# Turning keys on VectorE and through DRAM instead of on TensorE, in a four-block transformer kernel

## The chip, the cores and the metric

One core of a Trainium2 chip runs the whole program. The core has five engines with instruction streams of their own: TensorE (PE, matmuls; its weight loads are shown as PEld), VectorE (DVE), ScalarE (ACT), GpSimd (POOL) and SyncE (SP). SP computes nothing; it issues most of the DMAs, in order. TensorE reads SBUF and writes PSUM (8 banks of 128 partitions x 512 floats); the other engines bring results out of PSUM.

The metric is device time in microseconds (us). The kernel before takes 925.78 us (median of three runs, 925.47 to 926.54).

## The reference

The input x is 2 batches of 1024 tokens with 512 features, in float32. Four blocks follow each other, each applied to the layer-normed running sum and added to it:

1. attention a: 4 heads of 128, in chunks of 128 tokens (the stage that the change touches most);
2. a gated feed-forward net (called f in the kernel), 512 to 1408 to 512, whose weights are integer codes;
3. attention b: full softmax attention over 1024 tokens;
4. the same feed-forward net once more (called g).

Attention a, cut to what matters, for each batch, chunk and head:

```
q, k, v = x@Wq + bq, x@Wk + bk, x@Wv + bv
k = k / max(|k|, 1e-12)
attn  = (q k^T) * beta^T * decay        # decay is causal, from cumulative log gates
y     = attn v  +  (q state^T) * chunk_decay
state = state * total_decay + v^T (k * beta * decay_to_end)
```

The product q k^T contracts over the 128 features of a head. TensorE contracts over partitions, so the keys, which come out of their projection with tokens on partitions, are needed a second time with features on partitions: kT, a 128x128 transpose for each head.

## The kernel before, in words

**Tiling.** The 2048 tokens are 16 tiles (t = 0 to 15) of 128 tokens, and 4 groups (st = 0 to 3) of 4 tiles. Matmul inputs that need float32 accuracy are cut into a high and a low part, hi by a ScalarE cast and lo by a VectorE subtraction (`split`, L73), and multiplied in three matmuls (`mm3`, L88).

**Attention a** is the loop over t from L749. One turn does, in the order of the code: one head of the queries of a later group (`q_head`, L500, four turns ahead, so turns 0 to 11 have one and 12 to 15 have none); the keys and values of tile t+1 (`kv_tile`, L577, which calls `kv_part` for Wk and for Wv); and `scores(t)` (L617). `scores` turns the keys of tile t with four TensorE transposes into one PSUM bank (pkT, L622), copies them to SBUF with ScalarE (kT, L624), squares the keys of t+1 for their norm (`k_norm`), does the state's products (pd, L635), finishes tile t-1 (`chunk_out`: pl, L668, and pg, L673), and multiplies kT by the queries (pS, L650). Every fourth turn has the gates' projection as well (`gate_proj`, pc). The tiles kT and the keys (sWk) have two buffers each.

**Layer norms.** Groups 0 and 1 of attention a are turned by TensorE (`layernorm_T`). All later norms (groups a2, a3, f0 to f3, b0 to b3 and g0 to g3, 14 groups in all) go another way: `ln_norm` (L188) normalises a tile and turns its 32x32 blocks with VectorE (L198) into the tile y, which has one buffer; `ln_move` (L201) then puts the blocks on their partitions with 16 DMAs for each group, from SBUF to SBUF, each of 32 partitions x 16 x 32 floats (L209). The groups a, f, b0, b1, half of b2 and g3 are issued by SP, the others by POOL. `ln_split` (group a) and `combine` (the others) then read the turned group and make the matmul inputs, in slots of a pool of 12 (`slot`, L50). In `ln_split` the low part is written over the turned group.

The same kind of move through DRAM already stands in attention b: the probabilities are turned in 32x32 blocks by VectorE (L1100), written to DRAM by one DMA (L1104) and read back by four DMAs that put the blocks in place (L1116).

**What sets the order.** The code's order gives priorities. A planner with its own model of times then orders each engine's instructions and SP's DMAs ahead of the run, and puts in the waits; on the chip every engine and every DMA queue runs its list strictly in that order. `behind(...)` and `tc.issue_after(...)` add orders by hand: what is in their block comes after a given instruction of the same engine. `key_copy` holds such an instruction, the ScalarE copy of kT: the decay of tile t+1 (`decay`, ScalarE and POOL), the casts of groups a2 and a3 (`a_split`, at t = 3 and 7) and the squares of `k_norm` stand behind it.

**The end of attention a.** From t = 12 the loop also prepares the next block: `combine("f", 0)` in `moving` (subtractions L257, splits L76), the weight product V (its operands are loaded at L82 and split; pV), and the first feed-forward weights. The feed-forward net's products are pX, pY, pZ and pV with the suffix f or g.

Of the kernel before, what the change touches and what calls it, by code (L numbers as in the profile page):

```python
# [16 lines left out]
P = 128  # L17
D = 512
KD = D // P
# [15 lines left out]
def hybrid_block_kernel(ctx: ExitStack, tc: tile.TileContext, a, out):  # L35
# [14 lines left out]
    def slot(name, dt=F32R):  # L50

        return wp.tile([P, 2048], dt, tag="slot", name=name)
# [20 lines left out]
    def split(hi, lo, src, eng=None):  # L73

        c = nc.scalar.copy(hi, src)  # L75
        return c.ins, (eng or nc.vector).tensor_tensor(lo, src, hi.bitcast(F32), ALU.subtract).ins  # L76
# [61 lines left out]
    x_in = a["x"]  # L138
    x1 = [dp.tile([P, D], F32, tag=f"x1_{t}", name=f"x1_{t}") for t in range(NT)]
    x2 = [dp.tile([P, D], F32, tag=f"x2_{t}", name=f"x2_{t}") for t in range(NT)]  # L140
    x3 = [dp.tile([P, D], F32, tag=f"x3_{t}", name=f"x3_{t}") for t in range(NT)]
    cl_d = [dp.tile([16, P], F32, tag=f"cl_{g}", name=f"cl_{g}") for g in range(NST)]
    p_d = [dp.tile([T // P, P, P], F32, tag=f"p_{i}", name=f"p_{i}") for i in range(NC)]
# [39 lines left out]
            low.dma_start(out=dst[m][:, 512:1024], in_=lo.bitcast(F32))  # L183
        return done

    lnT, lnY, lnX, laid = {}, {}, {}, []

    def ln_norm(src, nm, st, i):  # L188

# [10 lines left out]

    def ln_move(nm, st, b):  # L201

        if b == 0:
            lnT[nm, st] = slot(f"xT_{nm}{st}").rearrange("p (k c) -> p k c", k=KD)
        y = lnY[nm, st]
        xf = lnT[nm, st].bitcast(F32).rearrange("p k (i b q) -> p (k i) b q", i=ST, b=4)
        for c in range(4):
            sync = nm in "af" or (nm, st) in (("b", 0), ("b", 1), ("g", 3)) or ((nm, st) == ("b", 2) and c % 2)
            (nc.sync if sync else nc.gpsimd).dma_start(  # L209
                out=xf[32 * b : 32 * (b + 1), :, c, :],  # L210
                in_=y[32 * c : 32 * (c + 1), b].rearrange("p k i q -> p (k i) q"),
            )

    def ln_split(nm, st):

        def part(k):
            if k == 0:
                xl = lnT[nm, st]
                lnT[nm, st] = slot(f"xh_{nm}{st}").rearrange("p (k c) -> p k c", k=KD), xl
            xh, xl = lnT[nm, st]  # L220
            split(xh[:, k, :], xl[:, k, :], xl[:, k, :].bitcast(F32))

        return [lambda k=k: part(k) for k in range(KD)]

# [17 lines left out]
    def combine(nm, pr):  # L242


        B = {}

        def begin():
            ra, rb = (lnT[nm, 2 * pr + n].bitcast(F32) for n in range(2))
            B.update(B11=ra[:, 0:2], B12=rb[:, 0:2], B21=ra[:, 2:4], B22=rb[:, 2:4])

        def part(n, src):
            o = slot(f"{n}_{nm}{pr}").rearrange("p (s k c) -> p s k c", s=2, k=2)
            XT[nm, pr, n] = o
            split(o[:, 0], o[:, 1], B[src])

        def less(dst, x, y):
            nc.vector.tensor_tensor(B[dst], B[x], B[y], ALU.subtract)  # L257

        if nm == "b":

            return [
                lambda: (begin(), part("B11", "B11")),
                lambda: part("B21", "B21"),
                lambda: part("B12", "B12"),
                lambda: part("B22", "B22"),
                lambda: less("B11", "B12", "B11"),
                lambda: part("T1", "B11"),
                lambda: less("B12", "B22", "B12"),
                lambda: part("T3", "B12"),
                lambda: less("B22", "B22", "B11"),  # L270
                lambda: part("T2", "B22"),
                lambda: less("B21", "B21", "B22"),
                lambda: part("T4", "B21"),
            ]
# [73 lines left out]
    with ExitStack() as actx:  # L348
# [16 lines left out]

        wc = a1.tile([P, KD, 2, 384], F32R, name="wc")
        normed, key_copy, late_norm = {}, [], []
        xTa, za, gta, sca, qTa, kva, ata, deca, sta, rowa, facta = ({} for _ in range(11))
        wqkv = {}
        rows = a1.tile([P, 2 * D + 96], F32, name="rows")  # L370
        bk_b, bv_b, bab_b = rows[:, 0:D], rows[:, D : 2 * D], rows[:, 2 * D : 2 * D + 2 * H]
# [186 lines left out]
        def kv_part(t, nm):  # L558
            st, i = divmod(t, ST)
            xh, xl = xTa[st]  # L560
            cs = bass.ts(i, P)
            ps = psum(f"p{nm}{t}")
            n = 256 if nm == "Wv" else 512
            for k in range(KD):
                w = wqkv[nm][k]
                mm3(ps[:, 0:n], xh[:, k, cs], xl[:, k, cs], w[:, 0:n], w[:, n : 2 * n], k == 0, k == KD - 1)
            if nm == "Wv":
                o, b = av.tile([P, 2, P], F32, tag="sWv", name=f"sWv{t}"), bv_b[:, 0:256]
            else:
                o, b = tl("sWk", t), bk_b  # L570
            nc.vector.tensor_tensor(o.rearrange("p h d -> p (h d)"), ps[:, 0:n], b, ALU.add)
            kva[t] = (*kva.get(t, ()), o)
# [1 line left out]
        def value(t, h):  # L574
            return kva[t][-1][:, h, :] if h < 2 else vbs[0][:, t % 8, h - 2, :]

        def kv_tile(t):  # L577
            kv_part(t, "Wk")
            kv_part(t, "Wv")

        def k_norm(t, after=None):

            kf, v = kva[t]
            sq = tl("sq", t)
            ss = mp.tile([P, H], F32, tag="ss", name=f"ss{t}")
            with tc.issue_after(after) if after is not None else nullcontext():
                for h in range(H):
                    squared = nc.scalar.activation(
                        sq[:, h, :], kf[:, h, :], AF.Square, accum_out=ss[:, h : h + 1]
                    ).ins  # L590
            normed[t] = (squared,)
            if t == NT - 1:
                late_norm.append(lambda: k_factor(t, ss))
            else:
                k_factor(t, ss)
# [21 lines left out]
        def scores(t):  # L617
            st, i = divmod(t, ST)
            kf, kw, v = kva[t]
            pkT = psum(f"pkT{t}").rearrange("p (h c) -> p h c", h=H)  # L620
            for h in range(H):
                nc.tensor.transpose(pkT[:, h, :], kf[:, h, :], ident)  # L622
            kT = tl("kT", t)
            copied = nc.scalar.copy(kT, pkT).ins  # L624
            key_copy[:] = [copied]
            if t == 0:
                with behind((copied,)):
                    decay(0)
            if t + 1 < NT:
                k_norm(t + 1, copied)  # L630
            if kw is not None:
                ec = sca[st][1]
                pd = psum(f"pd{t}").rearrange("p (h c) -> p h c", h=H)
                for h in range(H):
                    nc.tensor.matmul(pd[:, h, :], kw[:, h, :], value(t, h), start=True, stop=True)  # L635
                new = tl("state", t, pool=av)
                if t % NC == 0:
                    nc.vector.tensor_copy(new, pd)
                else:
                    old = tl("sdec", t)  # L640
                    nc.gpsimd.tensor_tensor(
                        old, sta[t], ec[:, 2, i, :].unsqueeze(2).to_broadcast([P, H, P]), ALU.mult
                    )
                    nc.vector.tensor_tensor(new, pd, old, ALU.add)
                sta[t + 1] = new
            if t > 0:
                chunk_out(t - 1)
            pS = psum(f"pS{t}").rearrange("p (h c) -> p h c", h=H)
            for h in range(H):
                nc.tensor.matmul(pS[:, h, :], kT[:, h, :], qTa[st][:, h, bass.ts(i, P)], start=True, stop=True)  # L650
            at = tl("at", t)
            s1 = facta.pop(t)
            for h in range(H):
                weighed = nc.vector.scalar_tensor_tensor(
                    at[:, h, :], pS[:, h, :], s1[:, h : h + 1], deca[t][:, h, :], ALU.mult, ALU.mult
                ).ins
            ata[t] = at
            return weighed
# [66 lines left out]
                with behind((*normed_x, *copied)):  # L725
                    spill(ap, ("kT", "kw", "sdec", "at"), pm, m_d, "M")
        load_wv()
        kv_tile(0)
        decays(0)
        k_norm(0)  # L730

# [15 lines left out]
        moving = combine("f", 0)  # L747
        wcs, loads = [], []
        for t in range(NT):  # L749
            if t + 4 < NT:  # L750
                q_head(*divmod(t + 4, ST))
            if t == 0:
# [2 lines left out]
                load_row(1)  # L755
            load_row(t + 1)
            if t + 1 < NT:
                kv_tile(t + 1)
            weighed = scores(t)
            if t % ST == 0 and t + ST < NT:  # L760
                gate_proj(t // ST + 1)
# [40 lines left out]
                next(prep)  # L802
        next(prep)
        chunk_out(NT - 1)
        spilled = spill(ap, ("sq", "kT", "kw", "sdec"), next(prep)[0], vo_d, "V")


    def ffn(src, dst, nm, wcs, moving, ended, after):
# [532 lines left out]
```

## Time and profile before

| what | value |
|---|---|
| median of three runs | 925.78 us (925.47 to 926.54) |
| profiled execution, its own time | 925.62 us |
| its span, first to last instruction | 923.9 us |
| granted TensorE clock | 1.000 |
| PE busy | 918.3 us (99%), 4546 matmuls |
| DVE busy | 692.0 us (75%) |
| ACT busy | 434.1 us (47%) |
| POOL busy | 260.2 us (28%) |
| DMA packets | 216182, of them 151024 under 512 bytes |

The page of a profile gives the busy time of each engine, the span in 40 slices, the DMA queues, the chain of work that ended last, and the costliest groups of instructions. A group is a source line, an engine and an operation with its tiles; a mean is the time of one instruction from its start to its end. Matmuls overlap their neighbours, so what one costs in a row of them is the distance between starts and not its own duration. Further answers of the trace are used below: who waited for whom, one tile's instructions, the chain in order of time, and stretches of the timeline of one engine or queue. SPq is the queue of DMAs that SP issues. The time of a DMA has two parts: how long SP is taken up by issuing it, and how long after that the data have landed.

### The profile page before, as it was taken

To read this page: it belongs to the slowest core of one execution; us is meant where nothing else is said; L and a number is where in the kernel's file an instruction comes from. 1 tells how busy PE (TensorE), PEld (TensorE's weight loads), DVE (VectorE), ACT (ScalarE), POOL (GpSimd) and SP (SyncE) were. 2 spreads that over 40 slices of the span, in tenths; PEclk is the share of its full clock that TensorE was granted. 3 is DMA by queue.
4 is the path that set the end of the run, shared out by engine and by line. 5 is a ranking of instruction groups with operands and counts; after the bars stand their busy time and mean duration, and the time that the engine had idled before them with its cause. 6 is when DMAs were issued, how large, how long until landed. Compare 5 with 4: busy or idle time off the path is not lost.

```text
span 923.9 us, 13662 instructions
## 1 busy us (share of the span) xinstructions
PE 918.3 (99%) x4546; PEld 778.6 (84%) x4546; DVE 692.0 (75%) x1335; ACT 434.1 (47%) x928; POOL 260.2 (28%) x458
## 2 busy tenths in 40 slices
PE   9999999999999999999999999999999999999998
PEld 8899999998888888888888888888888888888887
DVE  7755657579998798788948878569978876977654
ACT  5645455556776434444234444145444444444431
POOL 4345334556563002212130401140501531001100
PEclk9999999999999999999999999999999999999999
DMA  9535655477979754724743779225969745454012
GB/s 324 190 104 123 208 160 152 145 209 272 370 223 329 214 177 156 212 49 139 278 99 77 171 175 260 71 43 130 247 144 366 241 146 137 165 206 140 20 69 80
DMA packets 216182, 162.20 MB, mean 176 GB/s; under 512 B 151024, under 2 KB 167728, under 8 KB 216112
## 3 DMA queue, kind: packets, MB, share of 16 engines
q1 hardware_dynamic: 212624, 150.05, 53.6%
q0 software_dynamic: 3488, 11.28, 4.6%
q8 instruction: 36, 0.59, 0.3%
q14 instruction: 34, 0.28, 0.1%
HBM read 104.76 MB, written 41.84 MB: 159 GB/s over the span
## 4 chain that ended last, share of the span: by engine, by line
PE 93%; DVE 2%; SPq 2%; DMA 2%; issue 1%; ACT 0%; POOL 0%; DVEq 0%; ACTq 0%
PE pog L925 4%; PE pog L924 4%; PE pXf L338 4%; PE pVg L338 4%; PE pXg L338 4%; PE pof L924 4%; PE pVf L338 4%; PE pZf L338 4%; PE pZg L338 4%; PE pof L925 4%; PE pob L90 3%; PE pob L89 3%; PE pob L91 3%; PE psZ L1023 2%; PE psV L1023 2%; PE psX L1023 2%
## 5 line engine op out<-in xcount | busy, mean ns | idle before, releaser
L924 PE MATMUL pog<-wdg,hsg 128*128 128x512 f32 (+1 forms) x165 | 60.1, 375 | 0.0
L925 PE MATMUL pog<-wdg,hsg 128*128 128x512 f32 (+1 forms) x165 | 60.0, 375 | 0.0
L925 PE MATMUL pof<-wdf,hsf 128*128 128x512 f32 x154 | 59.1, 389 | 0.0
L924 PE MATMUL pof<-wdf,hsf 128*128 128x512 f32 x154 | 58.9, 389 | 0.0
L76 POOL TENSOR_TENSOR hsg<-sgg,hsg 128x128 fp32r<-128x128 f32 x40 | 18.6, 486 | 112.7 <-ACT hsg L75 68.8
L89 PE MATMUL pob<-vh,pth 128*128 128x512 f32 x128 | 49.9, 390 | 0.0
L91 PE MATMUL pob<-vh,ptl 128*128 128x512 f32 x128 | 49.8, 389 | 0.0
L90 PE MATMUL pob<-vl,pth 128*128 128x512 f32 x128 | 49.8, 389 | 0.0
L338 PE MATMUL pVg<-T_g,wcg 128*128 128x512 f32 x176 | 46.4, 389 | 0.0
L338 PE MATMUL pVf<-T_f,wcf 128*128 128x512 f32 x176 | 46.2, 389 | 0.0
L338 PE MATMUL pXg<-B_g,wcg 128*128 128x512 f32 x176 | 46.2, 389 | 0.0
L338 PE MATMUL pXf<-B_f,wcf 128*128 128x512 f32 x176 | 45.7, 390 | 0.0
L113 POOL TENSOR_SCALAR ve_g<-mv_g 128x1 f32<-128x1 f32 x16 | 8.0, 508 | 128.5 <-DVE mv_g L111 128.4
L209 POOL DMA_DIRECT2D xT_g<-y_g x48 | 31.1, 657 | 36.1 <-DVE T_b L76 29.4
L338 PEld LDWEIGHTS pVf<-T_f,wcf 128*128 128x128 f32 x176 | 33.0, 188 | 6.9
L338 PEld LDWEIGHTS pXg<-B_g,wcg 128*128 128x128 f32 x176 | 33.0, 188 | 6.8
L338 PEld LDWEIGHTS pVg<-T_g,wcg 128*128 128x128 f32 x176 | 33.0, 188 | 6.9
L338 PEld LDWEIGHTS pXf<-B_f,wcf 128*128 128x128 f32 x176 | 33.0, 188 | 6.8
L545 ACT ACTIVATE row<-row,ncl 128x128 f32<-128x128 f32 x64 | 20.5, 391 | 34.2 <-POOL row L534 34.1
L113 POOL TENSOR_SCALAR ve_b<-mv_b 128x1 f32<-128x1 f32 x16 | 5.6, 352 | 109.7 <-DVE mv_b L111 109.6
L924 PEld LDWEIGHTS pog<-wdg,hsg 128*128 128x128 f32 x165 | 31.1, 188 | 5.6
L925 PEld LDWEIGHTS pog<-wdg,hsg 128*128 128x128 f32 x165 | 31.0, 188 | 5.6
(344 smaller groups left out, 2844.2 us busy)
## 6 DMA issues: line engine op xcount, KB each, us to landing
wcg<-wc SPq DMA_DIRECT2D x19, 896.0 KB, 5.1
wc<-wcf SPq DMA_DIRECT2D x11, 896.0 KB, 5.1
p<-py SPq DMA_DIRECT2D x15, 512.0 KB, 3.6
wcf<-wc SPq DMA_DIRECT2D x8, 896.0 KB, 6.2
ptl<-p SPq DMA_DIRECT2D x56, 128.0 KB, 3.0
xin_a<-in_x SPq DMA_DIRECT2D x16, 256.0 KB, 4.9
xra<-in_x SPq DMA_DIRECT2D x16, 256.0 KB, 3.3
row<-cl SPq DMA_DIRECT2D x16, 256.0 KB, 4.1
```

The lines of the kernel that those rows point to most:

```text
L76: return c.ins, (eng or nc.vector).tensor_tensor(lo, src, hi.bitcast(F32), ALU.subtract).ins
L89: nc.tensor.matmul(ps, lhs_hi, rhs_hi, start=first, stop=False)
L90: nc.tensor.matmul(ps, lhs_hi, rhs_lo, start=False, stop=False)
L91: end = nc.tensor.matmul(ps, lhs_lo, rhs_hi, start=False, stop=last).ins
L113: nc.gpsimd.tensor_scalar(ve, mv[:, 1:2], EPS, None, ALU.add)
L209: (nc.sync if sync else nc.gpsimd).dma_start(out=xf[32 * b : 32 * (b + 1), :, c, :], in_=y[32 * c : 32 * (c + 1), b].rearrange("p k i q -> ...
L338: nc.tensor.matmul(ps, w[:, m, k * P : (k + 1) * P], o[:, s, k, :], start=first and k == 0 and s == 0, stop=k == 1 and s == 1, skip_group_ ...
L545: nc.scalar.activation(row[:, h, :], row[:, h, :], AF.Exp, bias=ncl[:, n : n + 1], scale=-1.0)
L924: nc.tensor.matmul(ps, hs[i][0][:, j], wd[j][:, ds], start=j == 0, stop=False)
L925: nc.tensor.matmul(ps, hs[i][1][:, j], wd[j][:, ds], start=False, stop=j == KH - 1)
L1023: ends[nm] = nc.tensor.matmul(ps, o[:, i, k], w[:, j, k], start=first and k == 0 and i + j == 0, stop=k == 1 and i == 1, skip_group_check= ...
```

## The change: what it does

1. Keys of tiles 1 to 11 (`TURNED`): the four TensorE transposes and the ScalarE copy are replaced by `turn_key`: one VectorE transpose of 32x32 blocks into a tile ky, one DMA to DRAM (k_d) and four DMAs back into kT, all five issued by SP. Tiles 0 and 12 to 15 stay as they were.
2. `kv_tile` is taken apart. The keys of t+1 (`k_tile`, with `turn_key`) now stand at the start of turn t, ahead of the later group's `q_head`; the values stand where they stood.
3. `key_copy` holds the VectorE transpose for the turned tiles, and `k_norm` of t+1 is no longer ordered behind the ScalarE copy.
4. All 14 norm groups: `ln_move` writes a group to DRAM with four DMAs (SP) and reads it back with one (SP for a and f, POOL for b and g). The slot for the group is taken only at the read. The group lies in another order in its slot, so `ln_split` and `combine` read it in runs of 32 floats; `ln_split` writes into two new slots.
5. The tiles sq (squares, two buffers before) and ky have one buffer each, and the V spill uses the buffers of `at` in place of those of sq.

```diff
+    k_d = [dp.tile([H, P, P], F32, tag=f"k_{t}", name=f"k_{t}") for t in range(NT)]
...
     def ln_move(nm, st, b):
         if b == 0:
-            lnT[nm, st] = slot(f"xT_{nm}{st}").rearrange("p (k c) -> p k c", k=KD)
-        y = lnY[nm, st]
-        xf = lnT[nm, st].bitcast(F32).rearrange("p k (i b q) -> p (k i) b q", i=ST, b=4)
-        for c in range(4):
-            sync = nm in "af" or (nm, st) in (("b", 0), ("b", 1), ("g", 3)) or ((nm, st) == ("b", 2) and c % 2)
-            (nc.sync if sync else nc.gpsimd).dma_start(
-                out=xf[32 * b : 32 * (b + 1), :, c, :],
-                in_=y[32 * c : 32 * (c + 1), b].rearrange("p k i q -> p (k i) q"),
+            lnD[nm, st] = dp.tile([P, 4, 512], F32, tag=f"ln_{nm}{st}", name=f"ln_{nm}{st}")
+        d = lnD[nm, st]
+        nc.sync.dma_start(
+            out=d.rearrange("(b q) c f -> c q b f", b=4)[b],
+            in_=lnY[nm, st][32 * b : 32 * (b + 1)].rearrange("p b k i q -> p b (k i q)"),
+        )
+        if b == 3:
+            lnT[nm, st] = slot(f"xT_{nm}{st}")
+            (nc.sync if nm in "af" else nc.gpsimd).dma_start(
+                out=lnT[nm, st].bitcast(F32), in_=d.rearrange("p c f -> p (c f)")
             )
 
     def ln_split(nm, st):
         def part(k):
             if k == 0:
-                xl = lnT[nm, st]
-                lnT[nm, st] = slot(f"xh_{nm}{st}").rearrange("p (k c) -> p k c", k=KD), xl
-            xh, xl = lnT[nm, st]
-            split(xh[:, k, :], xl[:, k, :], xl[:, k, :].bitcast(F32))
+                lnD[nm, st] = lnT[nm, st].bitcast(F32).rearrange("p (c k i q) -> p k i c q", c=4, k=KD, i=ST)
+                lnT[nm, st] = new_xT(f"{nm}{st}")
+            hi, lo = (x[:, k].rearrange("p (i c q) -> p i c q", i=ST, c=4) for x in lnT[nm, st])
+            split(hi, lo, lnD[nm, st][:, k])
...
     def combine(nm, pr):
         def begin():
-            ra, rb = (lnT[nm, 2 * pr + n].bitcast(F32) for n in range(2))
-            B.update(B11=ra[:, 0:2], B12=rb[:, 0:2], B21=ra[:, 2:4], B22=rb[:, 2:4])
+            ra, rb = (
+                lnT[nm, 2 * pr + n].bitcast(F32).rearrange("p (c n q) -> p n c q", c=4, q=32) for n in range(2)
+            )
+            B.update(B11=ra[:, 0:8], B12=rb[:, 0:8], B21=ra[:, 8:16], B22=rb[:, 8:16])
         def part(n, src):
...
-            split(o[:, 0], o[:, 1], B[src])
+            split(*(o[:, s].rearrange("p k (i c q) -> p (k i) c q", i=ST, c=4) for s in range(2)), B[src])
...
-        def kv_tile(t):
+        def turn_key(t):
+            y = tl("ky", t, pool=a1)
+            turned = nc.vector.transpose(
+                y.rearrange("p h c -> p (h c)"), kva[t][0].rearrange("p h c -> p (h c)")
+            ).ins
+            key_copy[:] = [turned]
+            nc.sync.dma_start(out=k_d[t].rearrange("h p f -> p h f"), in_=y)
+            kTa[t] = kT = tl("kT", t)
+            placed = k_d[t].rearrange("h (c j) (r q) -> r j (h c) q", c=4, r=4)
+            for n in range(4):
+                nc.sync.dma_start(
+                    out=kT[32 * n : 32 * (n + 1)].rearrange("p h (c q) -> p (h c) q", c=4), in_=placed[n]
+                )
+
+        TURNED = range(1, NT - 4)
+
+        def k_tile(t):
             kv_part(t, "Wk")
-            kv_part(t, "Wv")
+            if t in TURNED:
+                turn_key(t)
 
         def k_norm(t, after=None):
             kf, v = kva[t]
-            sq = tl("sq", t)
+            sq = tl("sq", t, pool=a1)
...
         def scores(t):
             kf, kw, v = kva[t]
-            pkT = psum(f"pkT{t}").rearrange("p (h c) -> p h c", h=H)
-            for h in range(H):
-                nc.tensor.transpose(pkT[:, h, :], kf[:, h, :], ident)
-            kT = tl("kT", t)
-            copied = nc.scalar.copy(kT, pkT).ins
-            key_copy[:] = [copied]
+            if t not in TURNED:
+                pkT = psum(f"pkT{t}").rearrange("p (h c) -> p h c", h=H)
+                for h in range(H):
+                    nc.tensor.transpose(pkT[:, h, :], kf[:, h, :], ident)
+                kTa[t] = tl("kT", t)
+                key_copy[:] = [nc.scalar.copy(kTa[t], pkT).ins]
+            kT = kTa.pop(t)
             if t == 0:
-                with behind((copied,)):
+                with behind(key_copy):
                     decay(0)
             if t + 1 < NT:
-                k_norm(t + 1, copied)
+                k_norm(t + 1)
...
-        kv_tile(0)
+        k_tile(0)
+        kv_part(0, "Wv")
...
         for t in range(NT):
+            if t + 1 < NT:
+                k_tile(t + 1)
             if t + 4 < NT:
                 q_head(*divmod(t + 4, ST))
...
             if t + 1 < NT:
-                kv_tile(t + 1)
+                kv_part(t + 1, "Wv")
             weighed = scores(t)
...
-        spilled = spill(ap, ("sq", "kT", "kw", "sdec"), next(prep)[0], vo_d, "V")
+        spilled = spill(ap, ("at", "kT", "kw", "sdec"), next(prep)[0], vo_d, "V")
```

More of the change, by code (lines that the diff above doesn't have):

```diff
@@ L184, in spill @@
         return done
-    lnT, lnY, lnX, laid = {}, {}, {}, []
+    lnT, lnY, lnX, lnD, laid = {}, {}, {}, {}, []
     def ln_norm(src, nm, st, i):
@@ L367, in hybrid_block_kernel @@
         normed, key_copy, late_norm = {}, [], []
-        xTa, za, gta, sca, qTa, kva, ata, deca, sta, rowa, facta = ({} for _ in range(11))
+        xTa, za, gta, sca, qTa, kva, ata, deca, sta, rowa, facta, kTa = ({} for _ in range(12))
         wqkv = {}
```

## The prediction

> **What bounds the kernel now.** I read the page first: busy times, then the chain that ended last.
>
> ```profile
> PE 918.3 (99%) x4546; PEld 778.6 (84%) x4546; DVE 692.0 (75%) x1335; ACT 434.1 (47%) x928; POOL 260.2 (28%) x458
> PE 93%; DVE 2%; SPq 2%; DMA 2%; issue 1%; ACT 0%; POOL 0%; DVEq 0%; ACTq 0%
> ```
>
> TensorE is busy nearly all of the span, and 93% of the chain lies on it. A busy PE can hide stalls inside overlapping matmuls, so the second view is PE's own list of waits:
>
> ```profile
> PE warm L685 <- POOL ones L356: 1.3, 1, 1.3
> PE pS L650 <- ACT kT L624: 0.3, 1, 0.3
> PE pl L668 <- DVE at L654: 0.2, 1, 0.2
> PE pM L89 <- ACT M L75: 0.2, 1, 0.2
> ```
>
> In the whole span PE waits 2.0 us, and after its start only twice. So the time is the sum of the distances between PE's starts: whatever leaves PE's list is gained in full, provided that no new wait comes in.
>
> **What the transposes cost.** Third view, the tile pkT, and two steps of the chain in order of time:
>
> ```profile
> L622 PE MATMUL pkT<-ident,sWk x64: 270/273/274, 49.1 to 217.3; 128*128 128x128 f32 x64
> L624 ACT COPY kT<-pkT x16: 562/586/588, 49.7 to 220.9; 128x512 f32<-128x512 f32 x16
> ...
> 64.29 0.44 PE pkT L622 x4
> 64.72 0.89 PE pd L635 x8
> ```
>
> One transpose lasts 273 ns, but the four of a tile hold PE for 0.44 us, some 110 ns each, before pd starts. Eleven tiles: 11 x 0.44 = 4.8 us of PE.
>
> Here a page of the Trainium skill differs in size: TensorE: Matmul & The Clock Gate, Part 4: PE-mode transpose, puts a 128x128 transpose at about 275 ns in a kernel. That is the duration in the row, and as a price 44 x 0.275 would make 12.1 us. The starts 110 ns apart decide; I take 4.8.
>
> ScalarE loses 11 copies x 0.58 = 6.4 us, which gain nothing where it is 47% busy. VectorE gets 11 transposes of 128x512. The row of the same operation, y_b at L198, has 700 ns: 11 x 0.70 = 7.7 us over the stretch from 50 to 190 us, where VectorE is 5 to 7 tenths busy. They lie beside PE's work; without that cover, 0.70 us for each tile.
>
> A second rule speaks against the change: VectorE: DVE Perf Modes, Rules for kernel authors, sends a 128x128 transpose to TensorE if PSUM will do as its destination. By that rule the change is wrong by 4.8 us or more; the waits above say that TensorE is the scarce engine here.
>
> **The new chain to kT.** After the keys' last matmul: VectorE adds the bias (sWk, L571, 0.68 us, which may queue up to 2.7 us, as at 112.5 to 115.2 us), turns (0.70), SP writes, SP waits until that has landed, SP issues four reads, the last lands. Attention b has this pattern with tiles twice as large:
>
> ```profile
> L1104 SPq DMA_DIRECT2D p<-py x15: 365/371/508, 499.5 to 683.3; - x15
> DMA to landing us min/median/max: 3.0/3.6/6.3
> ...
> L1116 SPq DMA_DIRECT2D ptl<-p x56: 303/563/2602, 502.5 to 675.4; - x56
> DMA to landing us min/median/max: 2.1/3.0/5.4
> ```
>
> Write 0.37, landing 3.0 to 3.6, four reads 4 x 0.6 = 2.4, landing 3.0: with VectorE's 1.4 this is 10.2 to 10.8 us, and with its queue 13.
>
> The cover is what PE does between the two. With the keys at the head of the turn, from the end of Wk(t+1) to pS(t+1) PE does, by the timeline from 118 to 139 us: in turn t pq 2.8, pWv 1.4, pd, pl, pg and pS 0.9 each (7.8); in turn t+1 Wk 2.7, pq 2.8, pWv 1.4, pd, pl and pg 2.7 (9.6). That is 17.4 us, a pd less in a batch's last chunk, and 5.9 more with pc. Slack is 4.4 to 7 us. The range stops at tile 11, the last with a later group's queries in both turns: without those 5.6 us the cover would be 11.8, below the 13.
>
> **SP's queue.** In order, one DMA at a time: a read that waits for its write holds up all that stands behind it (rows of decay, xra loads and stores, xin). Today the norm groups do that, as the timeline of SP shows:
>
> ```profile
> 75.19 11.94 SPq L209 DMA_DIRECT2D xT_a<-y_a  x16
> 87.23 0.56 SPq L680 DMA_DIRECT2D x<-xra  x1
> ...
> 186.47 6.73 SPq L209 DMA_DIRECT2D xT_f<-y_f  x8
> 193.31 0.56 SPq L680 DMA_DIRECT2D x<-xra  x1
> 193.91 5.33 SPq L209 DMA_DIRECT2D xT_f<-y_f  x8
> ...
> 200.94 0.42 SPq L82 DMA_DIRECT2D stg_Vl<-in_WvT  x1
> ```
>
> Four groups (a2, a3, f0, f1) fall between 75 and 200 us: 64 issues of 0.63 to 0.75, some 12 us a group, 48 together. New for them: 4 x 5 issues of rows of 2 KB or more, 0.33 to 0.43 each (as xin, x<-xra), 8 us, and 4 waits of 3 us. New for the keys: 11 x (0.37 + 2.4) = 30 us and 11 waits of 3 us. SP issues 38 us in place of 48 and waits up to 45 us more; its other work, some 2 us a turn, is as before. In a turn of 10.6 us (11.05 today between pkT at 125.35 and 136.40, less 0.44) that makes 2.8 for keys, 3 waiting, 2 others, 0.7 of norms, and 1 for a group's landing: 9.5. SP gets fuller evenly, but its longest block, 12 us, goes. Beside blocks of 12 us PE waits only 0.3 and 0.2 us today; I book 0 for SP, with 0 to 5 us of lateness as the ends, which the slack takes. The buffers add no wait: ky (one) is free again when its write has landed, some 6 us before the next turn's transpose, and kT (two) when pS(t-1) ends, just before Wk(t+1) begins.
>
> **The norms' way.** After the last y of a group: today 16 issues (12) and a landing of 2.1, 14 us. New: four writes 1.7, landing 2.3 to 3.6, a read of 1 MB, by the 896 KB rows of wc 0.35 and 5.1 to 6.2 to landing: 9.5 to 12. Each group is ready 2 to 4.5 us sooner. On POOL 72 DMAs x 0.66 = 47 us become 8 x about 0.6; nothing waits for POOL there. The b and g groups give SP up to 4 writes more, behind y, where it now has gaps. Packets of 128 bytes fall by 152 x 512 = 78 thousand; keys add 11 x 2048.
>
> The reads in runs of 32 floats: bound from below by L855 (strided, 745 ns) against L1144 (dense, 745): nothing; from above by y at L198 (runs of 32, 700 ns) against half of L1100 (620): 0.08 us per 512 floats. On some 66 operations of 1024 that is at most 10 us of VectorE under 580 us of PE work. I take 0. The extra slot in `ln_split` is there: Wq, Wk, Wv and vb take 6, the living pair 2, the group 1, the new pair 2: 11 of 12. sq with one buffer costs nothing, as ScalarE writes it in order.
>
> **Where a stall could come next: the end of attention a.** PE reaches the feed-forward net 4.8 us sooner and needs T_f and V sooner.
>
> ```profile
> 190.00:200.00 10.00, 10.00 (x71) 9.22 (x70) 5.99 (x14) 3.98 (x14) 6.40 (x11) 1.00 0.66 125
> 200.00:210.00 10.00, 10.00 (x78) 9.50 (x77) 7.91 (x17) 6.68 (x19) 6.06 (x9) 1.00 0.91 306
> 210.00:220.00 10.00, 10.00 (x67) 8.95 (x66) 10.00 (x20) 8.98 (x25) 3.53 (x7) 1.00 0.79 273
> ```
>
> Columns are PE, PEld, DVE, ACT, POOL busy, clock, DMA share, GB/s. From 210 us VectorE is full; from 189 to 207 it idles 6 us, partly for xT_f (1.42) and for V's operand (1.14), both behind SP's block of f1. That block shrinks from 12 to some 5 us, so these operands come 4 us or more sooner, and 6 us of idle time can take up the 4.8. Cost booked: 0; ends 0 and 4.8.
>
> **Sum.** 925.62 (the profiled execution: a span of 923.9 and 1.7 around it, 0.16 below the median) - 4.8 + 0.2 for small new gaps of the kind that stand today = 921.0 us; best case, if both of today's gaps (0.5) go too, 920.3.
>
> **Rivals.**
>
> - *The end of attention a swallows it.* For: VectorE full from 210 us on, DMA share 0.91. Against: the 6 us of idle time just before. Price: half of the 4.8 gives 923.4, all of it 925.8.
> - *Slower: kT comes late through SP.* Each read waits in SP's list behind a write's landing and behind stores that wait for VectorE (L680, up to 7.2 us in SP's waits). If SP's backlog adds 6 us to the chain's 13, kT comes 19 - 17.4 = 1.6 us late; times 11 is 17.6, less 4.8: 938.6. It decides from a mean lateness of 0.44 us a tile (4.8 / 11). For: SP at 9.5 of 10.6 us. Against: the cover of 17.4, and today's blocks of 12 us beside waits of 0.3.
> - *The order.* The planner lays out every engine anew; PE's list today leaves 0.5 us of gaps after the start, and another order need not. If it leaves 6 us, 927.
> - *The copy was hidden anyway*: true of ScalarE's 6.4 us, not of PE's, since PE has no wait to give back. I give this nothing.
>
> **How the numbers follow.** Whole gain 0.58; end swallows it 0.13, half of that faster, half no change; kT late 0.22; order 0.07, slower. A measurement tells about 0.2%, 1.9 us, from no change. Faster 0.58 + 0.06 = 0.64, same 0.07, slower 0.29. The likeliest case's own range is 920 to 922.5; the range to 929 takes in the swallowed gain and mild lateness (0.7 us a tile), and leaves out about 0.17 above and 0.03 below.
>
> **What would show it.** Right: pkT in 5 tiles (20 matmuls), PE busy about 913.5 us, the first pXf near 222.5 instead of 227.2 us, PE's waits after the start below 1 us, SP free of blocks of 12 us. Wrong: PE waits at pS for a DMA into kT (the slower rival), at pXf or pV for VectorE (the end), or gaps spread over lines that the change doesn't touch (the order). If VectorE's sWk starts more than 4 us after Wk, the chain was sized wrongly.

## The result

The changed kernel takes 939.31 us (median of six runs, 937.05 to 941.05); the kernel before took 926.16 us beside it. The ratio is 1.0135, 95% interval [1.0113, 1.0158]: slower by 1.1 to 1.6%. The forecast was 921.0, its range reached up to 929.0, and "slower" had a chance of 0.29.

What was meant to happen on TensorE did happen. The busy and chain lines of the page, and the tile pkT (min/median/max ns, first and last start):

```profile
PE 919.3 (98%) x4502; PEld 777.6 (83%) x4502; DVE 700.4 (75%) x1346; ACT 429.0 (46%) x917; POOL 212.6 (23%) x394
PE 85%; DMA 6%; POOL 3%; ACT 2%; DVE 2%; issue 1%; SPq 1%; POOLq 0%; ACTq 0%; DVEq 0%
...
L649 PE MATMUL pkT<-ident,sWk x20: 270/272/273, 49.2 to 231.4; 128*128 128x128 f32 x20
```

44 matmuls are gone (4546 to 4502) and pkT is left in five tiles. But the chain that ended last was 93% PE and is now 85%, with DMA 6% and POOL 3%. The list of PE's waits (total us, times, longest) was 2.0 us long; now:

```profile
PE pS L677 <- ACT kT L651: 6.2, 1, 6.2
PE pc L89 <- DVE sWv L578: 3.3, 1, 3.3
PE warm L712 <- POOL ones L363: 1.3, 1, 1.3
PE pl L695 <- DVE at L681: 1.2, 1, 1.2
PE pcum L488 <- ACT qT L526: 1.2, 1, 1.2
PE pr L502 <- DVE mv_f L111: 1.0, 1, 1.0
PE pS L677 <- DMA kT<-k: 0.9, 1, 0.9
PE pof L954 <- ACT hsf L75: 0.7, 1, 0.7
```

Two things are to be seen. The wait that the slower rival named, pS for a DMA into kT, is there once, with 0.9 us. The big ones are elsewhere: pS(12) waits 6.2 us for ScalarE's copy of a key that TensorE turned, and pc waits 3.3 us for VectorE to empty a bank. With the halved clock that follows (last section), the distances between PE's starts exceed the usual ones by some 20 us, nearly all between 75 and 225 us. Span: 939.1 - 923.9 = 15.2, that is some 20 lost and 4.8 won.

The longest one, followed back. ScalarE's and GpSimd's timelines (start, duration, then what ended the idle time before):

```profile
204.60 1.28 ACT L552 ACTIVATE row<-row,ncl 128x128 f32<-128x128 f32 x4 [8.83 <-POOL row L541]
...
207.88 0.57 ACT L651 COPY kT<-pkT 128x512 f32<-128x512 f32 x1
```

```profile
203.93 0.64 POOL L541 TENSOR_SCALAR_AFFINE_SELECT row<-row 128x512 f32<-128x512 f32 x1 [5.21 <-DMA row<-cl]
```

The key was turned by 199.6 us, but ScalarE's list has the decay of tile 12 ahead of the copy, and the decay waits for rows that come through DRAM. Why they came late stands in the timelines of SP and of VectorE:

```profile
187.18 1.91 SPq L595 DMA_DIRECT2D kT<-k  x4
...
192.67 0.80 SPq L209 DMA_DIRECT2D ln_f<-y_f  x2
193.56 0.83 SPq L505 DMA_DIRECT2D cl<-clr  x1
194.45 2.24 SPq L209 DMA_DIRECT2D ln_f<-y_f  x2
...
197.39 1.17 SPq L314 DMA_DIRECT2D wd<-cf  x1
198.67 0.91 SPq L560 DMA_DIRECT2D row<-cl  x2
```

```profile
184.78 0.69 DVE L109 BATCH_NORM_STATS2 bn_f<-xin_f 128x6 f32<-128x512 f32 x1 [7.49 <-DMA xin_f<-x]
...
193.14 0.26 DVE L504 COPY clr<-pr 16x128 f32<-16x128 f32 x1
```

PE had made the row (pr) at 186.6. VectorE copies it out of PSUM (clr) only at 193.1: its list had stood 7.5 us for a row of x until 184.8, and other work stood ahead of the copy. SP sends the row to DRAM at 193.6 and asks for it back at 198.7, behind writes and loads; it lands 5.2 us later. In the kernel before, pr, the sending and the asking were at 177.7, 181.4 and 183.5. So from pr to the asking it took 5.8 us before and 12.1 now: of the 6.3 more, 3.3 lie ahead of the sending, with VectorE, and 3.0 behind it, with SP.

SP's own waits between 40 and 245 us, first the seven largest of the kernel before, then some of the changed one:

```profile
SPq L664 <- DMA x<-xra: 14.6, 7, 4.8
SPq L307 <- ACT cf L302: 13.4, 6, 3.7
SPq L680 <- DVE xra L677: 10.6, 2, 7.2
SPq L680 <- DVE at L654: 10.1, 7, 3.3
SPq L498 <- DVE clr L497: 8.2, 3, 6.8
SPq L102 <- ACT xn_f L120: 7.1, 6, 4.1
SPq L102 <- ACT e L456: 6.4, 1, 6.4
```

```profile
SPq L691 <- DMA x<-xra: 22.4, 8, 7.3
SPq L595 <- DMA k<-ky: 18.3, 9, 3.7
...
SPq L591 <- DVE ky L587: 8.2, 2, 8.0
```

So SP already stood 70 us in these seven groups, waiting for others' work or for landings. The keys add 18.3 us for landings and 8.2 for VectorE (8.0 of it in one wait), and the wait for the residual's stores grows from 14.6 to 22.4. Other waits shrink. Added up over the whole view, SP's waits for landings go from 24.4 to 51.4 us and those for other engines from 83.9 to 57.9; all together they are 108.3 before and 109.3 now.

### The profile page after: what moved, and what is told of

It reads as the page before. It is cut to its first block, busy times and chain, and to the rows that moved or that the text cites. A ratio compares the mean times of both kernels' runs of the same rounds, so it can differ in the third digit from the quotient of the medians.

```text
span 939.1 us, 13474 instructions
## 1 busy us (share of the span) xinstructions
PE 919.3 (98%) x4502; PEld 777.6 (83%) x4502; DVE 700.4 (75%) x1346; ACT 429.0 (46%) x917; POOL 212.6 (23%) x394
## 4 chain that ended last, share of the span: by engine, by line
PE 85%; DMA 6%; POOL 3%; ACT 2%; DVE 2%; issue 1%; SPq 1%; POOLq 0%; ACTq 0%; DVEq 0%
PE pog L955 4%; PE pog L954 4%; PE pof L954 4%; PE pof L955 4%; PE pXf L345 4%; PE pXg L345 4%; PE pZg L345 4%; PE pVf L345 4%; PE pZf L345 4%; PE pVg L345 4%; PE pob L91 3%; PE pob L90 3%; PE pob L89 3%; PE psZ L1053 2%; PE psX L1053 2%; PE psV L1053 2%
## 5 line engine op out<-in xcount | busy, mean ns | idle before, releaser
L954 PEld LDWEIGHTS pof<-wdf,hsf 128*128 128x128 f32 x154 | 28.9, 188 | 7.1 <-ACT hsf L75 1.1
L955 PEld LDWEIGHTS pof<-wdf,hsf 128*128 128x128 f32 x154 | 28.9, 188 | 6.0
```

Of the source, the lines that this page charges most:

```text
L954: nc.tensor.matmul(ps, hs[i][0][:, j], wd[j][:, ds], start=j == 0, stop=False)
L955: nc.tensor.matmul(ps, hs[i][1][:, j], wd[j][:, ds], start=False, stop=j == KH - 1)
```

## The experiments

Three theories were set against each other. SyncE's list: issues, and waits at its head, make rows of x, of the decay and of the residual late, and the in-order engines then sit on the late one. Fuller DMA engines: the added traffic makes every landing later. Order: the planner's new lists put work that waits for a late load ahead of urgent work. Differences below are between medians, against runs of the kernel before made beside them (926.38 in the first group, then 927.03, 926.34 and 925.90).

**The two halves of the change, and two mends.**

e1_norms is the kernel before with the diff's changes to `ln_move`, `ln_split` and `combine` alone; e2_keys has all the others. e3_nowait and e4_decay are the changed kernel with:

```diff
-            placed = k_d[t].rearrange("h (c j) (r q) -> r j (h c) q", c=4, r=4)
+            placed = k_d[max(t - 1, 1)].rearrange("h (c j) (r q) -> r j (h c) q", c=4, r=4)
```

```diff
-            if t == 0:
+            if t in (0, NT - 4):
                 with behind(key_copy):
-                    decay(0)
+                    decay(t)
...
-            if t + 1 < NT:
+            if t + 1 < NT and t + 1 != NT - 4:
```

> Only the norms' part of the change (before, with all 14 groups placed through DRAM; keys turned by TensorE as before). SP list (SyncE's in-order queue is too full, so that loads behind it come late): the norms free SP of its blocks of 12 us, PE's list is that of before, 924.5 to 926.5 us. DMA engines (the transfers themselves crowd each other): the same, as the norms' share of the 16 engines hardly grows, 925 to 928. Order (the planner's new order puts late work ahead of urgent work): the norms alone change no key order, 925 to 927.

> Only the keys' part (before, with keys 1 to 11 turned by VectorE and through DRAM at the head of the turn; norms placed from SBUF to SBUF with 16 DMAs a group). SP list: the keys' five DMAs a turn meet the norms' blocks of 12 us on SP, so it is at least as slow as the whole change, 938 to 948 us. DMA engines: 935 to 942. Order: 930 to 940, since the ScalarE copy no longer holds back the decay.

> The whole change, but kT of tile t (2 to 11) is read from the DRAM tile of t-1, which was written a turn earlier: the same transfers, but SP no longer waits for the write that it has just issued. The output is not the reference's: tiles 2 to 11 use the keys of the tile before in q k^T. SP list: the 18.3 us that SP waits at L595 for k<-ky go, and what stands behind comes sooner: 926 to 933 us. DMA engines: the transfers are the same, 937 to 941. Order: 936 to 941.

> The whole change, with one order put right: the decay of tile 12 stands behind the ScalarE copy of kT of tile 12, the first one that TensorE turns again. Order: the 6.2 us wait of pS(12) for the copy, and the slow clock after it (some 2 us), go: 929 to 933 us. SP list and DMA engines: the row of tile 12 is as late as before and its decay only moves its wait to another instruction, part of it hidden: 931 to 938 us.

| run | us | against before | ratio, 95% |
|---|---|---|---|
| e1_norms | 933.06 | +6.7 | [1.006, 1.009] |
| e2_keys | 943.01 | +16.6 | [1.0165, 1.0205] |
| e3_nowait | 933.75 | +7.4 | [1.0067, 1.0097] |
| e4_decay | 934.84 | +8.5 | [1.0068, 1.011] |

The norms' part, which every theory had taken for harmless, loses 6.7 us by itself. With the keys in, it helps (e2 is 3.7 us slower than the full change); it spares SP 44 issues in the four groups of attention a, which may be why. e4 takes the decay out of the copy's way: the 6.2 us wait is gone, yet only 4.5 us are won, less than the theory of order had expected.

e3 is 5.6 us better than the changed kernel, just outside the range of SyncE's list and well below the other two. But it changes more, and less, than was expected. SP's wait for the write falls only by half:

```profile
SPq L595 <- DMA k<-ky: 9.0, 4, 3.2
```

The reads now stand earlier in SP's list, and four of them still wait for the write of the tile before. And kT no longer depends on the key of its own turn, so that it is ready much sooner. So e3 alone does not give the price of the landing wait.

How e1 loses is a case of order, with a late load. VectorE's timeline in the kernel before, then in e1:

```profile
91.16 0.67 DVE L109 BATCH_NORM_STATS2 bn_a<-xin_a 128x6 f32<-128x512 f32 x1
91.75 1.30 DVE L76 TENSOR_TENSOR xT_a<-xT_a,xh_a 128x512 fp32r<-128x512 f32 x2
```

```profile
96.18 0.70 DVE L109 BATCH_NORM_STATS2 bn_a<-xin_a 128x6 f32<-128x512 f32 x1 [2.56 <-DMA xin_a<-in_x]
96.79 1.28 DVE L76 TENSOR_TENSOR xl_a<-xT_a,xh_a 128x512 fp32r<-128x512 f32 x2
```

Both times ScalarE casts the new group at 88.8 us. But in e1 the split stands behind two statistics of the next norm, and the second waits for a row of x that SP issued at 89.8, having stood 4.5 us for a residual store to land. PE waits 3.0 us for the split.

**More mends, and the order by itself.** g1_a3late changes e1 by one line; g3_fix puts the same line into e4_decay. g2_keypool is the changed kernel with the five key transfers on `nc.gpsimd` in place of `nc.sync`. g4_order is e2_keys with `TURNED = range(0)`.

```diff
-            (xa, "a", 3, (2, 2, 3, 4, 4, 5, 5, 5)),
+            (xa, "a", 3, (4, 4, 4, 5, 5, 5, 6, 6)),
```

> The kernel before with the norms' part of the change alone, and with the norms of x's group 3 given out to tiles 4 to 6 in place of tiles 2 to 5, so that VectorE's list has the four splits of group 2 ahead of group 3's statistics (in the norms' part alone, 933.06 us, it had them behind, and the statistics waited for a row of x). The theory of order (work that waits for a late load is set ahead of urgent work in an in-order list): the wait of 3.0 us for the split and the halved clock behind it go, 925 to 928.5. The theories of SyncE's list and of the fuller DMA engines: the transfers are the same, 931 to 934.

> The changed kernel with the keys' five transfers of a tile issued by GpSimd in place of SyncE: the same bytes and packets, and SyncE's list is as short as it would be without them. The theory of SyncE's list: rows of the decay, of x and of the residual come earlier, 927 to 935. The theory of fuller DMA engines: nothing changes, 937 to 941. A rival: GpSimd's own list, which now waits for the key block's landing ahead of the mask of the decay and of the key factors, makes these late, 940 to 955.

> The changed kernel with two mends of order and nothing else: the decay of tile 12 behind the copy of its turned key (alone: 934.84 us), and the norms of x's group 3 given out to tiles 4 to 6 in place of 2 to 5. The theory of order: both late splits go, 926 to 931.5. The theory of SyncE's list: the loads are as late as before and find other victims, 932 to 936.

> The kernel before with the keys' product alone moved ahead of the later group's queries; TensorE turns all keys, no key goes through DRAM, the norms are placed as before. What the new order costs by itself. The theory of SyncE's list and that of fuller DMA engines: no more transfers than before, 924.5 to 928. The theory of order: the planner sets other work ahead of urgent work here too, 930 to 936.

| run | us | against before | ratio, 95% |
|---|---|---|---|
| g1_a3late | 931.26 | +4.2 | [1.0027, 1.0071] |
| g2_keypool | 943.87 | +16.8 | [1.0154, 1.0193] |
| g3_fix | 941.50 | +14.5 | [1.0132, 1.0171] |
| g4_order | 930.93 | +3.9 | [1.0023, 1.0052] |

The theory of order does not explain the whole loss. g1 has the splits ahead of the statistics and wins 2.5 us by the differences, with intervals that overlap. g3 has both mends and is no better than the changed kernel, above both expectations: pl now waits 5.3 us, pr 1.8. The lateness found other victims. But an order has a price. g3 is 6.7 us slower than e4 with the same transfers, and g4, which does the old work with the old transfers, loses 3.9 us, as the theory of order had it and the others had not. PE's largest wait in g4 is this:

```profile
PE pS L671 <- ACT kT L645: 4.4, 2, 2.7
```

Of the two, 1.7 us are at tile 3, whose key the change turns elsewhere, and 2.7 at tile 12, where TensorE still turns it. So the 3.9 us cannot be carried over to the changed kernel as they are.

g2 does not decide between the other two, because GpSimd's list became the late one, as its rival had it: it waited 12.3 us for VectorE's ky before the write, and 13.1 us for rows of the decay. Its largest stall shows how long a landing can get:

```profile
PE pq L89 <- ACT xh_a L75: 6.1, 1, 6.1
```

The read of group a2 was issued at 89.56 and ScalarE's cast began at 98.96; from 85 to 95 us the DMA engines' share was 0.91 to 0.94.

**Issues, wait and bytes apart.** Here the changed lists are left out altogether: the kernel before gets dummy transfers in `kv_tile`, after the keys of tiles 1 to 11, whose data nobody uses. The lists of the engines stay almost as they were (the matmuls' list differs in one stretch of a turn); between d4 and d1 those of PE, ScalarE and GpSimd are the same. This is d1_sp; d5_both reads `k_d[t]` instead, the block just written. d4_issue and d2_wait are the same pair with 8 KB written and 4 x 2 KB read. Two things are not as with real keys: the reads go to DRAM and not to SBUF, and tile 1 reads its own block, so that d4 and d1 wait for a landing once (2.5 and 3.7 us).

```diff
+        def load_alone(t):
+            put = nc.sync.dma_start(out=k_d[t].rearrange("h p f -> p h f"), in_=kva[t][0]).ins
+            read = k_d[max(t - 1, 1)].rearrange("h (c j) (r q) -> r j (h c) q", c=4, r=4)
+            with behind((put,)):
+                for n in range(4):
+                    nc.sync.dma_start(
+                        out=j_d[t][32 * n : 32 * (n + 1)].rearrange("p h (c q) -> p (h c) q", c=4), in_=read[n]
+                    )
```

> The kernel before, its order of work nearly unchanged, with five dummy transfers on SyncE's queue for each of tiles 1 to 11, where the key tile is ready: 8 KB of the key into DRAM, and four reads of 2 KB of the block of the tile before, which has long landed. SyncE issues as many transfers as for the turned keys, but waits for no landing, and hardly a byte moves. First of four runs that set the number of issues, the wait and the bytes apart. Theory of SyncE's list: some 2.3 us of issuing a turn out of 14, 926 to 931. Theory of fuller DMA engines: nothing, 925 to 927.5.

> As the run with tiny dummy transfers, but the four reads are of the block just written, so SyncE stands until it has landed (3 us or so a turn). Theory of SyncE's list: the wait is what makes rows of x, of the decay and of the residual late, 930 to 938, well above the run without it. Theory of fuller DMA engines: 925 to 927.5.

> As the first, but with the keys' full bytes and packets: 256 KB of the key written in 512 B packets, and four reads of the block of the tile before in 128 B packets, into DRAM, no wait for a landing. Theory of SyncE's list: as the first, 926 to 931. Theory of fuller DMA engines: the 18 per cent of their time that the keys take make every other landing later, 931 to 940.

> Full bytes and packets, and the wait for the landing: the whole load that the keys put on SyncE and the DMA engines, while TensorE still turns every key and no engine waits for the dummies. Theory of SyncE's list: as the tiny ones with the wait, 930 to 938. Theory of fuller DMA engines: as the full ones without it, 931 to 940. If both count: more than either alone, 936 to 945. If neither (what the changed kernel loses comes of its order of work, not of its transfers): 925 to 928.

| run | bytes | SP waits for landing | us | against before | ratio, 95% |
|---|---|---|---|---|---|
| d4_issue | few | no | 929.48 | +3.1 | [1.0026, 1.0073] |
| d2_wait | few | yes | 935.60 | +9.3 | [1.0088, 1.0118] |
| d1_sp | all | no | 934.98 | +8.6 | [1.0078, 1.0126] |
| d5_both | all | yes | 941.34 | +15.0 | [1.0149, 1.0183] |

Both remaining theories hold, each for its share: issues 3.1, the wait 6.1 more, the bytes 5.5 more, sum 14.7 against 15.0 measured. SyncE's list alone had 926 to 931 for d1, the fuller DMA engines alone 925 to 927.5 for d2, and both miss; d5 lies in the range that was set for both together. The shares are rough, since the intervals are 3 to 4.5 us wide (d4's goes from +2.4 to +6.8 us), and that the sum comes so close is partly luck. The wait in the two kernels that have it, from SP's waits (d2_wait, then d5_both):

```profile
SPq L582 <- DMA k<-sWk: 17.8, 9, 3.2
```

```profile
SPq L584 <- DMA k<-sWk: 20.2, 9, 4.0
```

Both are near the 18.3 us of the changed kernel. The bytes show in the stretch from 125 to 150 us (columns after the counts: clock, DMA share, GB/s), d4_issue ahead of d1_sp:

```profile
125.00:150.00 25.00, 25.00 (x174) 22.96 (x173) 17.35 (x41) 15.40 (x48) 11.21 (x23) 1.00 0.56 178
```

```profile
125.00:150.00 25.00, 20.92 (x123) 18.49 (x122) 11.65 (x31) 12.45 (x40) 9.10 (x21) 0.86 0.79 203
```

The share goes from 0.56 to 0.79, PE stands for a sixth of the stretch (20.92 of 25.00 us busy), and the clock is 0.86. The lateness passes through four lists. The load of the next down weights (cd) is issued at 129.9 in place of 126.3 us and lands after 4.5; ScalarE's cf starts at 134.4 in place of 130.2; SP, which has to send cf on, issues the next row of x at 137.8 in place of 132.4; and VectorE's statistics wait for that row:

```profile
140.71 0.69 DVE L109 BATCH_NORM_STATS2 bn_f<-xin_f 128x6 f32<-128x512 f32 x1 [3.41 <-DMA xin_f<-x]
```

The keys' bias stands behind the statistics, ScalarE's squares wait for the bias until 142.3, and group 3's cast behind them starts at 143.5 in place of 138.8; pq waits 4.1 us for it. Not every landing is longer. Against the kernel before, the median for the residual goes from 3.3 to 3.9 us, for its store from 2.3 to 3.0 and for the rows of xin_a from 4.9 to 5.4, but for those of xin_f from 4.2 to 3.9. SP's issues are longer too: one of the dummy's reads takes 627 ns (median, 1984 at most) in place of 546.

One reserve: a dummy's write also waits in SP's list until VectorE has the key (6.3 to 6.5 us in d4 and d1), as the real one waits for ky. That wait is in the price of the issues, and nothing here splits it off.

**What was still open.** h1_readpool is e1_norms with every group's read on `nc.gpsimd`; h2_fbg is e1_norms with `ln_move` and `ln_split` of group a as before; h3_five is e2_keys with `TURNED = range(1, 6)`; h4_fix is e4_decay with h1's line.

> The norms' part alone, with the read of every group's block issued by GpSimd, so that SyncE no longer stands until the four writes of groups a and f have landed. If SyncE's wait for the landing is what costs (theory of SyncE's list): 926 to 930. If it is the 1 MB of more traffic a group (fuller DMA engines) or the new order of the splits: 930.5 to 934, as with SyncE's read (933.06).

> The norms' part for f, b and g alone; groups 2 and 3 of x go by sixteen transfers inside the chip's SBUF as before. If the loss lies in x's groups (late split, halved clock): 925 to 928. If f's groups, which are moved in the same stage of attention, cost as much: 929 to 932.

> The keys' part alone with tiles 1 to 5 turned by VectorE and through DRAM in place of 1 to 11. In proportion to the tiles (all eleven: 943.0; none, in the same order of work: 930.9), five would give 930.9 + 5/11 of 12.1, some 936.4, range 934.5 to 938.5. If SyncE's slack takes the first ones and only the fullest stretch breaks: 928 to 932.

> The changed kernel with the decay of tile 12 behind its key's copy (alone 934.84) and the norms' reads issued by GpSimd. Theory of SyncE's list: two waits of some 4 us a group less on SyncE, 929 to 933.5. Theory of fuller DMA engines: 933.5 to 937, since no byte is saved. Neither theory expects less than the kernel before: the keys' issues, wait and bytes alone cost 15 us against a gain of 4.8 on TensorE.

| run | us | against before | ratio, 95% |
|---|---|---|---|
| h1_readpool | 930.39 | +4.5 | [1.003, 1.0067] |
| h2_fbg | 928.03 | +2.1 | [1.0012, 1.0031] |
| h3_five | 930.04 | +4.1 | [1.0028, 1.0062] |
| h4_fix | 937.56 | +11.7 | [1.0103, 1.015] |

The groups of x carry most of the norms' loss: without them it falls from 6.7 to 2.1 us, of which 0.7 us is a wait at pof near 440 us that all kernels with the new norms share and that was not followed up. Taking SP's landing wait out of the norms (h1) lands between the two expectations; whether it helps stays open. Nor does it help the changed kernel: h4 is no faster than e4 and lies just above both expectations. h3 shows that the loss is not in proportion; it lies where it should if SyncE's slack takes the first tiles. With no tile through DRAM, but the same code order, it was +3.9; five tiles make it +4.1, gaining 2.2 on TensorE (5 x 0.44, not measured) and so losing about as much; six more make it +16.6. Among those five, the slower rival's own wait appears, once:

```profile
PE pS L671 <- DMA kT<-k: 3.0, 1, 3.0
```

No run beats the kernel before, and none points to a version that would: in the dummies the bytes alone cost 5.5 us, and all eleven tiles can give 4.8.

## Why the prediction was wrong, point by point

- **What bounds the kernel** (PE, 2.0 us of waits): right. The conclusion "whatever leaves PE's list is gained in full, provided that no new wait comes in" was right too, and the proviso decided.
- **TensorE's 4.8 us**: right in kind, 44 matmuls gone at 110 ns. No run measured the gain alone. VectorE's 7.7 and ScalarE's 6.4 us show nowhere in PE's waits by their duration: right.
- **The chain to kT, 10 to 13 us against a cover of 17.4**: wrong in its length, though that cost little. In the trace of the changed kernel the time from the end of Wk to the last landing in kT is 7.6 and 9.5 us for tiles 1 and 2, and 14.3 to 21.1 us for tiles 3 to 11. For tiles 5, 6, 8 and 9 VectorE's sWk starts 7.0 to 8.3 us after Wk, which by the prediction's own sign (more than 4) means that the chain was sized wrongly; for tiles 4, 7, 10 and 11 SP sends ky some 5 us after it is ready. The write lands after 4.0 us (median; 5.7 at most), where 3.0 to 3.6 was booked, a read after 2.6 (7.6 at most), where 3.0 was. PE still waited only 0.9 us in one tile of eleven, because it came late to pS itself, up to 27.4 us after Wk; in tiles 3, 4, 6 and 8 pS starts 0.2 us after kT has landed, so that nothing was left of the cover. e2_keys waited 5.7 us in three tiles.
- **SP's queue, "I book 0 for SP"**: the step that failed. The sum of 9.5 us in a turn of 10.6 was a mean load, and "0 to 5 us of lateness" was to be taken up by slack; the dummies measured issues and wait at +9.3 us (d2_wait). The view of SP's waits, printed above, was at hand: 70 us between 40 and 245 us, or 3.6 us in a turn. They are not load to be added to the 9.5, for they shrink when SP is late itself: in d5_both all waits for other engines come to 40.7 us, against 83.9 before, and five turned tiles cost hardly more than none (h3_five). So the queue had room on the mean. The waits point to something else: that SP often issues a load just when what it needs is ready, so that a delay ahead of it moves the load, and with it the engine that sits on it. d1 and e1 show one such case each, from load to stall; the prediction followed only kT.
- **Blocks of 12 us beside waits of 0.3 us** were the argument for slack, and it misled. That PE hardly waits beside four such blocks says that the loads behind them had slack, in the order of that kernel; it does not say what a wait in every turn costs, in another order.
- **The DMA engines** were not in the sum at all, and that is the second step that failed. The prediction counted that packets of 128 bytes fall; the keys' packets take 18% of the engines' time between 64 and 205 us (their packets' own times added up), the engines' share there, 0.33 to 0.68 by stages before, becomes 0.67 to 0.82, and the bytes cost 5.5 us in the dummies.
- **The norms, "each group is ready 2 to 4.5 us sooner"**: wrong. From a group's last y to its last landing, the four groups of attention a took 13.5, 13.2, 13.7 and 14.3 us before, and 12.1, 11.9, 12.5 and 15.7 in e1_norms: three 1.2 to 1.4 us sooner, one later. The cast of group a2 comes at 88.8 us as before, and what follows it is later. In the changed kernel the median landings of attention a's groups were 4.6 us for the writes and 6.7 for the read, not 2.3 to 3.6 and 5.1 to 6.2.
- **The end of attention a, cost 0**: right as far as it goes. PE waits nowhere at pXf or pV for VectorE, but it came to pXf at 241.0 us, not 222.5, so the case was never put to the test.
- **The rivals.** "kT comes late through SP" gave 938.6 and 939.3 was measured; that the two agree is luck. Its chain was right (19 us; 18.0 to 19.0 in tiles 3 to 8) and so was the queue. But its price stood on 1.6 us of waiting for kT in each of eleven tiles, and PE waited 0.9 us in one. SP's lateness fell on the loads behind the keys, whose slack the prediction never worked out. "The order" was given 6 us and 0.07: a new order alone measured 3.9 us in g4, and the chance was far too low.

In all, the keys' parts are -4.8 (TensorE, not measured alone), +3.9 (order, as g4 had it) and +15.0 (transfers, as the dummies had them), together 14.1 where the keys alone measured +16.6; the rest may be PE's own waits for kT, which the dummies cannot have. That the norms then take 3 us off again, while costing 6.7 alone, shows that these terms do not simply add in the full kernel.

## What to carry to other kernels

Before an in-order queue is given more work, look at its waits as well as at its issues in the stage concerned. That it has room on the mean does not settle it: here a turn had 9.5 us of work in 10.6 by the sum, five turned tiles cost next to nothing beyond the new order (h3_five), and eleven, order included, 16.6 us (e2_keys). Price a trip through DRAM at the landing of every other load in that stage, not only at its own chain, and ask which in-order engine sits on each late load and what urgent work stands behind. Where the engine that bounds the kernel waits almost nowhere, 5 us of its work are a poor bargain for eleven waits on a shared queue.

## What the runs showed of the hardware

**A short gap on TensorE can cost a third to a half as much again.** After the 3.3 us wait of the changed kernel at pc, the matmuls start 0.22 us apart instead of 0.12 for the next 3.4 us; after the 6.2 us wait, those of Wk start 0.43 apart instead of 0.23. The granted clock in these windows:

```profile
155.00:160.00 5.00, 2.44 (x11) 2.44 (x12) 3.70 (x11) 1.85 (x5) 2.89 (x5) 0.76 1.01 325
...
205.00:210.00 5.00, 1.49 (x7) 1.49 (x8) 1.99 (x3) 3.46 (x14) 2.70 (x4) 0.54 0.98 376
210.00:215.00 5.00, 5.00 (x24) 4.26 (x24) 5.00 (x11) 1.28 (x4) 3.05 (x4) 0.78 0.97 348
```

The two stalls of 9.5 us cost some 3.5 us more in this way. In d2_wait a wait of 2.6 us was enough: 1.1 us after its end, seven matmuls start 0.43 us apart. The length of the gap does not decide alone: in g3_fix a wait of 1.8 us was enough (clock 0.66 from 190 to 195 us), while in e2_keys the clock stayed at 1.00 about a wait of 2.4 us (185 to 195 us). The Trainium skill, TensorE: Matmul & The Clock Gate, Part 1: The HAM clock gate, has half rate follow after at least one idle window of about 3.4 us; the halving itself agrees, the gaps that brought it here were shorter.

**The same transfer lands after very different times.** The read of 1 MB that gives a group of norms its block lands after 5.3 and 8.2 us in attention a of the changed kernel, after 7.6 (median) in groups f and 5.3 in b. In g2_keypool, with a DMA share of 0.91 to 0.94, the data of one was used only 9.4 us after its issue. A 256 KB write of keys takes 4.0 us in the changed kernel (median), and one of the dummies of d5_both 3.6. With the dummies' bytes (d1_sp), the share from 125 to 150 us is 0.79 and the residual's store takes 3.0 us; in the kernel before, 0.55 and 2.3.
